# Folding the position-bias tiles of two steps into one of eight points with 16 rows each, ahead of the third layer of a small network

## The chip, the cores and the metric

The kernel runs on one core of a Trainium2 chip. The metric is the device time of one execution in microseconds (us); a comparison uses the median of several runs. Five engines work side by side, each through its own queue in order: PE (TensorE, matmuls into PSUM), DVE (VectorE), ACT (ScalarE), POOL (GpSimd) and SP (SyncE, which here only issues DMAs). DMAs are issued from SP's and POOL's queues and run on 16 DMA engines that all queues share; one that adds to its destination (an accumulating DMA) is issued from POOL. A trace of one profiled execution shows every instruction.

## The reference: what is computed

Four attention layers run one after the other on x of shape (2, 512, 32, 32), all in float32. Only the first, layer 0, is touched. It is a deformable attention: per image and group, 64 sampled key points, 1024 query pixels, and a bias that a small network (2 to 128 to 128 to 1) computes from the position of each query relative to each point:

```python
q = _gconv1x1(xn, qw)
...
pos = grid_q[:, :, None, :] - grid_kv[:, None, :, :]
bias = jnp.sign(pos) * jnp.log1p(jnp.abs(pos))
bias = jax.nn.relu(bias @ cpb_w1 + cpb_b1)
bias = jax.nn.relu(bias @ cpb_w2 + cpb_b2)
bias = (bias @ cpb_w3 + cpb_b3).reshape(b, GROUPS, H * W, Hd * Wd)
sim = jnp.einsum('bhid,bhjd->bhij', qh, kh) + bias
attn = jax.nn.softmax(sim, axis=-1)
out = jnp.einsum('bhij,bhjd->bhid', attn, vh)
...
out = jnp.einsum('bchw,oc->bohw', out, out_w) + out_b[None, :, None, None]
x = x + out
```

The network is evaluated 2 x 8 x 64 x 1024 times with 128 hidden units. Its second layer is a 128 x 128 product for each point and pixel, its third a product with one column.

## The kernel before

**Head pairs, steps and points.** Layer 0 works through 8 head pairs (`NT`; 2 images, 4 pairs of groups each, 128 points in a pair: one for each partition of `sim`). A pair has 32 *steps* (`NR`), a step 4 points, 256 steps in all (`steps`). For each point `first` (L491, one DVE instruction, L502) forms the 128 hidden values for 1024 pixels from two small tables, into a ring of 12 tiles of which 8 lie in the buffer `wa`; it runs 8 points (`AHEAD`, two steps) ahead of the step that uses them.

**Second layer.** `second` (L512) computes 32 of the 128 outputs (a *part*) for all four points at once: point p goes to rows 32p to 32p+31 of the PSUM tile `z`, so four matmuls of 32 columns run side by side in the array (L519). There are three `z` buffers, which all other small products of layer 0 share. ACT evicts `z` with the relu into an `h2` tile (L527). A step does the parts in the order 1, 0, 3, 2.

**Folding four parts into one.** The third layer is linear and has one output, so what follows the relu may be added up before it, if |w3| is multiplied into the second layer and the hidden units are sorted so that the sign of w3 is uniform over a row of a part. `joined` (L530) adds two parts on DVE, with a sign per row in `turn` (L532): part 0 takes in part 1 in the same step, part 2 takes in part 3 in the next step. An accumulating DMA on POOL's queue (L763) then adds the second sum onto the first. What remains of a step is one tile `joins[i]` of 128 rows: 4 points, 32 rows each.

**Third layer.** After every fourth step `third` (L537) multiplies the last four of these tiles with `w3`, a narrow matrix of signs whose slice `w3[:, 28 - r : 60 - r]` puts the four points of a tile on rows r to r+3 of a 32-row quarter of `sim`. Four tiles go to the four quarters, side by side, in two halves of 512 pixels: 8 matmuls (L542), each written as two records in the trace. 8 calls fill a pair's `sim`; then `scores` adds the attention scores, and `behind` (a chain of generators, advanced twice a step) does `finish` (softmax, L558), `offsets` (a depthwise convolution for the points of the pair after next, ACT products and DVE reduces, L310) and `samples` (L404) between the steps of the next pair.

**Order.** `in_order` keeps each engine's instructions in program order. The loop (L749) issues, for each of four k in a step: a `first`, a `second`, at k = 1 the join of the previous step and its DMA, at k = 1 and 3 one piece of `behind`, at k = 3 the join of this step. SP's queue has the table loads (`load_tabs`, L473, two every four steps, used from the second step of the next chunk on, after `scale_tab` on ACT) and the few other loads; after the last step also the 4 MB of `mlp_w1` (L751), which go into the buffer `wa`. POOL's queue has the accumulating DMAs and now and then a memset.

**Buffers.** `h2p` (8, part 0), `h2b` (3, part 2) and `h2q` (3, parts 1 and 3) hold the tiles. At the start the same pools hold weights (`qkwbd`, `nat`) for the *folds* (L690): products of weight matrices of a later layer that PE does before the steps begin.

**End of layer 0.** The last two steps are joined by DVE instead of the DMA (L765). `finish` of the last pair has nothing to hide behind; it does parts of the output projection (`project_out`, L624) for chunks 0 and 1 while the softmax runs, and the rest after.

Of the kernel before, what the change touches and what calls it, by code (L numbers as in the profile page):

```python
# [11 lines left out]
F32 = mybir.dt.float32  # L12
AF = mybir.ActivationFunctionType
ALU = mybir.AluOpType
AX = mybir.AxisListType
# [3 lines left out]
P = 128  # L19
B, C, H, W = 2, 512, 32, 32  # L20
HW = H * W
# [7 lines left out]
HID = 4 * C  # L29
EPS = 1e-5  # L30
BN_S = float(1.0 / np.sqrt(np.float32(1.0 + EPS)))
RCH = 4


_PC = [
# [44 lines left out]
def kernel(ctx: ExitStack, tc: tile.TileContext, a: dict, out: bass.AP):  # L80
# [56 lines left out]
    def layer0(l0, fold_d, t2_b, o2_b):  # L137
# [1 line left out]
        l0.enter_context(in_order(tc))  # L139
        one = l0.enter_context(tc.tile_pool(name="att1", bufs=1))  # L140
        two = l0.enter_context(tc.tile_pool(name="att2", bufs=2))
        h2p = l0.enter_context(tc.tile_pool(name="att_h2", bufs=8))
        h2b = l0.enter_context(tc.tile_pool(name="att_h2b", bufs=3))
        h2q = l0.enter_context(tc.tile_pool(name="att_h2q", bufs=3))
        dram = l0.enter_context(tc.tile_pool(name="l0dram", bufs=1, space=DRAM))
# [4 lines left out]
        def zt(shape, name):  # L150
            return ps_z.tile(shape, F32, name=name, tag="z")
# [10 lines left out]
        qkw = h2p.tile([P, 2, NPAIR, P], F32, name="qkwbd", tag="h2")  # L162
# [56 lines left out]
        b2h = one.tile([P, 4], F32, name="b2h")  # L219


        w3 = one.tile([P, 60], F32, name="w3")
        nc.gpsimd.memset(w3, 0.0)

        def magnitude(dst, src):
            nc.vector.tensor_scalar(dst, src, -1.0, None, ALU.mult)
# [2 lines left out]
        def bias_weights():  # L229
            sort = h2b.tile([P, 7, P], F32, name="sort", tag="h2")  # L230
            row, below, w2t = [sort[:, k, :] for k in range(3)]
            perm = sort[:, 3:, :].rearrange("p b (r u) -> p b r u", u=32)
            few = one.tile([P, 24], F32, name="few")
# [233 lines left out]
            nc.vector.tensor_add(simbias[t], pb, col("cpb_b3"))  # L467

        NR = 32
        NCH = NR // RCH  # L470
# [12 lines left out]

        def scale_tab(c, ax):
# [5 lines left out]

        def first(p):  # L491

            i, point = divmod(p, 4)
            chunk, quad = divmod(i, 4)
# [7 lines left out]
            nc.vector._custom_dve(  # L502
                TENSOR_ADD_SAT,
                out=h1.rearrange("p (y x) -> p y x", x=W),
                in0=tx[:, quad, point, :].unsqueeze(1).to_broadcast([P, H, W]),
                in1=ty[:, quad, point, :].unsqueeze(2).to_broadcast([P, H, W]),
                s0=float(np.finfo(np.float32).max),
                s1=0.0,
            )
            return h1  # L510

        def second(h1s, part):  # L512

            z = zt([P, HW], "z")
            lo = BLOCK[part]
            for half in range(2):
                n = slice(half * HALF, (half + 1) * HALF)
                for point in range(4):
                    nc.tensor.matmul(  # L519
                        z[point * 32 : point * 32 + 32, n],  # L520
                        cpb_w2[:, lo : lo + 32],
                        h1s[point][:, n],
                        start=True,
                        stop=True,
                    )
            h2 = (h2q if part % 2 else h2b if part else h2p).tile([P, HW], F32, name="h2", tag="h2")
            nc.scalar.activation(h2, z, AF.Relu, bias=b2h[:, part : part + 1])  # L527
            return h2

        def joined(parts, part):  # L530
            h2 = parts.pop(part)
            nc.vector.scalar_tensor_tensor(  # L532
                h2, h2, turn[:, part // 2 : part // 2 + 1], parts.pop(part + 1), ALU.mult, ALU.add
            )
            return h2

        def third(sim, r, h2s):  # L537

            for half in range(2):
                n = slice(half * HALF, (half + 1) * HALF)  # L540
                for quad, h2 in enumerate(h2s):
                    nc.tensor.matmul(  # L542
                        sim[quad * 32 : quad * 32 + 32, n],
                        w3[:, 28 - r : 60 - r],
                        h2[:, n],
                        start=(r == 0),
                        stop=False,
                    )

        def scores(t, sim):  # L550
# [3 lines left out]
                nc.tensor.matmul(sim[:, n], kqs[t], xs[b][:, pr, n], start=False, stop=True)  # L554

        oTs = {}

        def finish(t, sim):  # L558

# [29 lines left out]
            pps = []  # L589
# [22 lines left out]
            if pr < NPAIR - 1:  # L612
                return
            for m in range(CC):
                if m < len(pps):
# [133 lines left out]
        for i in range(steps + 2):  # L749
            if i == steps:  # L750
                (w1s,) = load_w(wa, "wa", [a["mlp_w1"]])  # L751
            for k, part in enumerate((1, 0, 3, 2)):
                if i % 4 == 1 and k % 2 == 0 and i // 4 + 1 in tabs_of:
                    scale_tab(i // 4 + 1, k // 2)
                p = 4 * i + AHEAD + k
                if p < 4 * steps:
                    h1s[p] = first(p)
                if i < steps:
                    parts.setdefault(i, {})[part] = second([h1s[4 * i + point] for point in range(4)], part)
                if k == 1 and i - 1 in parts:  # L760
                    other = joined(parts.pop(i - 1), 2)
                    if i < steps:
                        nc.gpsimd.dma_start(out=joins[i - 1], in_=other, accum_op=ALU.add)  # L763
                    else:
                        nc.vector.tensor_add(joins[i - 1], joins[i - 1], other)  # L765
                if k % 2:
                    next(behind, None)
                if k == 3 and i < steps:
                    joins[i] = joined(parts[i], 0)
            for point in range(4):  # L770
                h1s.pop(4 * i + point, None)
            if i >= 5 and i % 4 == 1:
                t, r = divmod(i - 5, NR)
                if r == 0:
                    sim = ps_s.tile([P, HW], F32, name="sim")
                third(sim, r, [joins.pop(i - 5 + j) for j in range(4)])
                if r == NR - 4:
                    assert next(behind, None) is None
                    scores(t, sim)
                    behind = chain(  # L780
                        finish(t, sim),
                        offsets(t + 2) if t + 2 < NT else iter(()),
                        samples(t + 1) if t + 1 < NT else iter(()),
                    )
        drain(behind)
        return w1s

# [856 lines left out]
```

## Time and profile before

| quantity | us |
| --- | --- |
| median of 3 runs | 3558.87 (3557.84 to 3559.7) |
| profiled execution | 3558.93 |
| span of its trace (first to last instruction) | 3556.6 |
| first matmul of the second layer (L519) starts | 61.9 |
| last one starts | 2061.0 |
| second layer on PE, busy (16384 records) | 1804.6 |
| third layer on PE, busy (1024 records) | 124.5 |
| second pair of heads, 32 steps (300.8 to 548.3) | 247.6, of which DVE busy 233.4, ACT 180.2 |
| `first` on DVE, each | 1.22 |
| join on DVE, each | 1.28 |

The kernel spends some 2000 us of its span in the steps of layer 0. "Busy" counts the time in which at least one instruction of a group runs, so four matmuls side by side count once. A wait in front of an instruction is given as idle time with the instruction that ended it (the releaser). Waits of PE are what sets the time here, as it is hardly ever idle.

### The profile page before, as it was taken

The page shows a single profiled execution, that of the slowest core. Times are in us where ns is not written, and L with a number is a line of the kernel's source. Part 1 is how long each engine was busy: PE and PEld are TensorE (multiplying, and loading weights), DVE is VectorE, ACT ScalarE, POOL GpSimd, SP SyncE. Part 2 cuts the span into 40 slices and gives each one's busy share as a digit, 9 for nine tenths or more (in the row PEclk, how much of TensorE's full clock was granted, in tenths as well). Part 3 has the DMA queues.
Part 4 walks back from the last instruction along what each step waited for, and adds up shares of the span by engine and source line. Part 5 has one row for each costly group of instructions (what it writes and reads, how often), then busy time and mean ns, then how long its engine had stood idle before and what let it go on. Part 6 is the DMA issues. An engine that isn't in the chain of part 4 may idle for free.

```text
span 3556.6 us, 58202 instructions
## 1 busy us (share of the span) xinstructions
PE 3522.7 (99%) x24777; PEld 1469.1 (41%) x24777; DVE 2479.0 (70%) x2720; ACT 1760.6 (50%) x2478; POOL 278.1 (8%) x326
## 2 busy tenths in 40 slices
PE   9999999999999999999999989999999999999999
PEld 4333333333333233333333349999533333444443
DVE  6999998998996998999999934554255364130223
ACT  4767866867764867767776621122144233111111
POOL 0111111111110111111111100000001000000000
PEclk9999999999999999999999999999999999999999
DMA  5454444554442444444444430000200000000000
GB/s 167 95 92 83 81 96 88 90 90 84 91 94 53 87 91 82 96 84 87 94 85 88 85 112 13 10 10 13 80 1 0 1 1 0 15 0 0 6 30 25
DMA packets 135964, 213.46 MB, mean 60 GB/s; under 512 B 14992, under 2 KB 93200, under 8 KB 134928
## 3 DMA queue, kind: packets, MB, share of 16 engines
q0 software_dynamic: 36720, 133.71, 19.9%
q1 hardware_dynamic: 98832, 75.41, 8.8%
q8 instruction: 197, 3.23, 0.4%
q14 instruction: 71, 0.58, 0.0%
q10 hardware_dynamic: 144, 0.52, 0.0%
HBM read 64.12 MB, written 10.75 MB: 21 GB/s over the span
## 4 chain that ended last, share of the span: by engine, by line
PE 96%; DVE 1%; ACT 1%; issue 1%; DMA 0%; POOL 0%; POOLq 0%; DVEq 0%; ACTq 0%
PE z L519 49%; PE pw L135 6%; PE pm L1243 5%; PE pma L135 5%; PE pmv L135 5%; PE pmb L135 4%; PE score L1354 4%; PE sim L542 3%; PE score L135 3%; PE pv L1402 3%; PE ppr L1274 2%; PE pmp L135 2%; PE pp L628 2%; PE pf L135 1%; PE pma L1216 1%
## 5 line engine op out<-in xcount | busy, mean ns | idle before, releaser
L527 ACT ACTIVATE h<-z,b2h 128x1024 f32<-128x1024 f32 x1024 | 1135.0, 1114 | 575.3 <-PE z L519 570.5
L519 PE MATMUL z<-wa,cpb_w 128*32 128x512 f32 x10880 | 1195.9, 593 | 3.3 <-ACT h L527 3.3
L502 DVE CUSTOM_DVE_ANT_1 wa<-tab,tab 128x1024 f32<-128x1024 f32 x680 | 801.1, 1221 | 23.6 <-PE z L519 19.5
L519 PEld LDWEIGHTS z<-wa,cpb_w 128*32 128x32 f32 x10880 | 346.4, 110 | 808.5 <-issue 730.8
L532 DVE SCALAR_TENSOR_TENSOR h<-h,turn,h 128x1024 f32<-128x1024 f32 x512 | 655.9, 1281 | 25.7 <-ACT h L527 25.6
L519 PE MATMUL z<-h,cpb_w 128*32 128x512 f32 x5504 | 608.7, 593 | 0.9 <-ACT h L527 0.9
L502 DVE CUSTOM_DVE_ANT_1 h<-tab,tab 128x1024 f32<-128x1024 f32 x344 | 405.3, 1221 | 15.0 <-PE z L519 14.9
L763 POOL DMA_DIRECT2D h<-h x255 | 219.5, 861 | 1801.2 <-DVE h L532 1308.8
L519 PEld LDWEIGHTS z<-h,cpb_w 128*32 128x32 f32 x5504 | 175.8, 110 | 408.4 <-issue 372.8
L1355 ACT ACTIVATE p<-score 128x1024 f32<-128x1024 f32 x144 | 139.6, 1021 | 184.8 <-PE score L1354 184.8
L135 PE MATMUL pw<-p,vT 128*128 128x512 f32 x512 | 221.8, 593 | 1.3 <-DVE y L1460 1.3
L1285 DVE TENSOR_TENSOR acc<-acc,p 128x2048 f32<-128x2048 f32 x56 | 128.8, 2300 | 105.1 <-ACT p L1355 57.8
L1138 ACT COPY p<-pma 128x128 f32<-128x128 f32 x70 | 18.6, 266 | 304.2 <-PE pma L135 304.2
L1287 DVE TENSOR_TENSOR acc<-p 128x2048 f32<-128x2048 f32 x12 | 27.5, 2292 | 183.6 <-ACT p L1489 110.0
L135 PEld LDWEIGHTS pw<-p,vT 128*128 128x128 f32 x512 | 97.0, 190 | 122.6 <-issue 121.0
L1130 DVE TENSOR_TENSOR upper<-pma,p 128x256 f32<-128x256 f32 x70 | 29.6, 423 | 163.5 <-ACT p L1138 163.5
L542 PE MATMUL sim<-h,w 128*32 128x512 f32 x1024 | 124.5, 598 | 5.8 <-DMA h<-h 5.8
L1354 PE MATMUL score<-q,k 64*128 64x512 f32 x512 | 127.2, 615 | 0.0
L1243 PE MATMUL pm<-hc,wa 128*64 128x512 f32 x512 | 122.4, 603 | 0.0
L1402 PE MATMUL pv<-p,vT 128*64 128x512 f32 x512 | 121.4, 595 | 0.0
L135 PE MATMUL score<-t,hc 128*128 128x512 f32 x256 | 110.2, 592 | 0.0
L1460 DVE TENSOR_TENSOR y<-pw,r 128x512 f32<-128x512 f32 x32 | 21.8, 682 | 115.5 <-PE pw L135 115.5
(300 smaller groups left out, 3110.2 us busy)
## 6 DMA issues: line engine op xcount, KB each, us to landing
h<-h POOLq DMA_DIRECT2D x255, 512.0 KB, 5.0
tab<-slog_d SPq DMA_DIRECT2D x128, 256.0 KB, 7.0
wa<-in_qkv_w SPq DMA_DIRECT2D x8, 768.0 KB, 6.2
xt<-in_xt SPq DMA_DIRECT2D x8, 512.0 KB, 5.8
wa<-in_mlp_w SPq DMA_DIRECT2D x4, 1024.0 KB, 9.7
wb<-in_mlp_w SPq DMA_DIRECT2D x16, 256.0 KB, 5.6
x_d<-x SPq DMA_DIRECT2D x32, 128.0 KB, 1.8
out<-x SPq DMA_DIRECT2D x16, 256.0 KB, 2.0
```

Of the source, the lines that this page charges most:

```text
L135: nc.tensor.matmul(pm, w, m, start=(k == 0), stop=(k == len(pairs) - 1))
L502: nc.vector._custom_dve(TENSOR_ADD_SAT, out=h1.rearrange("p (y x) -> p y x", x=W), in0=tx[:, quad, point, :].unsqueeze(1).to_broadcast([P, ...
L519: nc.tensor.matmul(z[point * 32 : point * 32 + 32, n], cpb_w2[:, lo : lo + 32], h1s[point][:, n], start=True, stop=True,)
L527: nc.scalar.activation(h2, z, AF.Relu, bias=b2h[:, part : part + 1])
L532: nc.vector.scalar_tensor_tensor(h2, h2, turn[:, part // 2 : part // 2 + 1], parts.pop(part + 1), ALU.mult, ALU.add)
L542: nc.tensor.matmul(sim[quad * 32 : quad * 32 + 32, n], w3[:, 28 - r : 60 - r], h2[:, n], start=(r == 0), stop=False,)
L763: nc.gpsimd.dma_start(out=joins[i - 1], in_=other, accum_op=ALU.add)
L1243: nc.tensor.matmul(pm[at : at + wide], w[:, k, lo + at : lo + at + wide], h[k][:, n], start=(k == 0), stop=(k == CC - 1),)
L1285: nc.vector.tensor_add(acc, acc, p)
L1354: nc.tensor.matmul(sc[:, part, :], ks[part][r, left[part]], qs[part][r, n], start=True, stop=True)
L1355: nc.scalar.activation(p[:, :, n], sc, AF.Exp, scale=scale)
L1402: nc.tensor.matmul(pv[part * 64 : part * 64 + 64, n], vT[:, ls, lo : lo + 64], lp[:, part, n], start=(ls == 0), stop=(ls == 7),)
```

## The change

A tile `joins[i]` has 4 points of 32 rows. The new kernel folds the 32 rows of a point into 16 and puts two steps into one tile: rows 2u get the sum of rows 2u and 2u+1 of the even step, rows 2u+1 the same sum of the odd step. Three transfers do it for each pair of steps (e even, o = e + 1):

- in step e + 2, at k = 0: an accumulating DMA on POOL's queue adds the odd rows of `joins[e]` onto its even rows (64 rows of 4 KB);
- in step e + 3, at k = 0: a DMA on SP's queue copies the even rows of `joins[o]` into the odd rows of `joins[e]`;
- in step e + 3, at k = 3: an accumulating DMA on POOL's queue adds the odd rows of `joins[o]` onto these.

The last two steps (254 and 255) aren't folded. `third` now takes four tiles of eight points each, with a sign matrix of 8 columns (`w3`, 56 wide); the last call takes three such tiles and the two tiles of four points through the old matrix (`w3_4`). It runs once for eight steps, at k = 1 of the third step after the last pair has begun its folds (`due`), instead of once for four steps after the fourth k. So `finish` of a pair begins a step and a half later too.

So that eight consecutive points fall into one tile, the tables are loaded in another order (`RCH` 8: two runs of 8 points for a chunk of 16 points, instead of four runs of 4), of the same size.

The pools: part 0 of even steps in `h2p` (now 6), of odd steps in a new pool `h2j` (3), which also holds `qkwbd` at the start.

At the top four small DVE operations build the new sign matrix, and one more piece of the folds goes ahead of the bias weights and the first offsets (`advance(fold_steps, 3)`). At the end the first two of four products of chunk 1's projection are issued right after the last step, and `finish` of the last pair keeps only chunk 0's early part; `pa` reuses `pt`'s buffer.

```diff
-RCH = 4
+RCH = 8
...
-        h2p = l0.enter_context(tc.tile_pool(name="att_h2", bufs=8))
+        h2p = l0.enter_context(tc.tile_pool(name="att_h2", bufs=6))
+        h2j = l0.enter_context(tc.tile_pool(name="att_h2j", bufs=3))
...
-                nc.vector.tensor_copy(w3[r, 28 + point : 29 + point], w3sign[r, 1:2])
+                nc.vector.tensor_copy(w3_4[r, 28 + point : 29 + point], w3sign[r, 1:2])
+
+            odd, eighth = few[:, 24:25], few[:, 25:26]
+            nc.vector.tensor_reduce(odd, ident[:, 1:P:2], AX.X, ALU.add)
+            nc.vector.scalar_tensor_tensor(eighth, odd, 4.0, cs("py", 0), ALU.mult, ALU.subtract)
+            nc.vector.tensor_scalar(w3[:, 24:32], row[:, 0:8], eighth, 0.0, ALU.add, ALU.is_equal)
+            nc.vector.tensor_scalar(w3[:, 24:32], w3[:, 24:32], w3sign[:, 1:2], None, ALU.mult)
...
-                tab = two.tile([P, 4, RCH, 32], F32, name=f"tab{ax}")
-                nc.sync.dma_start(out=tab, in_=src[:, rc * RCH : (rc + 1) * RCH, :].partition_broadcast(P))
+                tab = two.tile([P, 2, RCH, 32], F32, name=f"tab{ax}")
+                q, r = rc % 2 * 2, rc // 2 * RCH
+                nc.sync.dma_start(out=tab, in_=src[q : q + 2, r : r + RCH, :].partition_broadcast(P))
...
-            h2 = (h2q if part % 2 else h2b if part else h2p).tile([P, HW], F32, name="h2", tag="h2")
+            ring = h2q if part % 2 else h2b if part else h2j if i % 2 else h2p
+            h2 = ring.tile([P, HW], F32, name="h2", tag="h2")
...
-        def third(sim, r, h2s):
+        def third(sim, r, h2s, fours=()):
...
-                for quad, h2 in enumerate(h2s):
+                ways = [(quad, w3[:, 24 - r : 56 - r], h2) for quad, h2 in enumerate(h2s)]
+                for k, h2 in enumerate(fours):
+                    ways.append((3, w3_4[:, 28 - r - 4 * k : 60 - r - 4 * k], h2))
+                for k, (quad, w, h2) in enumerate(ways):
                     nc.tensor.matmul(
...
+                        sim[quad * 32 : quad * 32 + 32, n], w, h2[:, n], start=(r == 0 and k < 4), stop=False
                     )
...
-                pps = [zt([P, HW], "pp") for _ in range(2)]
-                for m in range(2):
-                    project_out(pps[m], m, range(NPAIR - 1 - m), oT)
-            pa = zt([P, 8, P], "pa")
+                pps.insert(0, zt([P, HW], "pp"))
+                project_out(pps[0], 0, range(NPAIR - 1), oT)
+            pa = pt if last else zt([P, 8, P], "pa")
...
-        advance(fold_steps, 2)
+        advance(fold_steps, 3)
...
             if i == steps:
                 (w1s,) = load_w(wa, "wa", [a["mlp_w1"]])
+
+                pps.append(zt([P, HW], "pp"))
+                project_out(pps[0], 1, range(NPAIR - 2), oTs[B - 1])
...
+                if i >= 2 and i % 2 == 0 and k == 0 and i < steps:
+                    nc.gpsimd.dma_start(out=joins[i - 2][0:P:2], in_=joins[i - 2][1:P:2], accum_op=ALU.add)
+                if i >= 3 and i % 2 and k == 0 and i < steps:
+                    nc.sync.dma_start(out=joins[i - 3][1:P:2], in_=joins[i - 2][0:P:2])
+                if i >= 3 and i % 2 and k == 3 and i < steps:
+                    nc.gpsimd.dma_start(out=joins[i - 3][1:P:2], in_=joins.pop(i - 2)[1:P:2], accum_op=ALU.add)
...
+                due = i - 11 if i < steps else i - 9
+                if k == 1 and due >= 0 and due % 8 == 0:
+                    t, r = divmod(due, NR)
...
+                    eights = [joins.pop(due + j) for j in range(0, 8 if i < steps else 6, 2)]
+                    third(sim, r, eights, [joins.pop(steps - 2 + j) for j in range(2)] if i >= steps else ())
+                    if r == NR - 8:
...
-            if i >= 5 and i % 4 == 1:
-                t, r = divmod(i - 5, NR)
...
-                third(sim, r, [joins.pop(i - 5 + j) for j in range(4)])
-                if r == NR - 4:
```

More of the change, by code (lines that the diff above doesn't have):

```diff
@@ L161, in layer0 @@
         nc.scalar.dma_start(out=xs[0][:, 0, :], in_=a["x"][0, 0:P, :])
-        qkw = h2p.tile([P, 2, NPAIR, P], F32, name="qkwbd", tag="h2")
+        qkw = h2j.tile([P, 2, NPAIR, P], F32, name="qkwbd", tag="h2")
         vw = one.tile([P, NPAIR, P], F32, name="vwbd")
@@ L219, in layer0 @@
         b2h = one.tile([P, 4], F32, name="b2h")
-        w3 = one.tile([P, 60], F32, name="w3")
-        nc.gpsimd.memset(w3, 0.0)
+        w3 = one.tile([P, 56], F32, name="w3")
+        w3_4 = one.tile([P, 60], F32, name="w3_4")
+        for w in (w3, w3_4):
+            nc.gpsimd.memset(w, 0.0)
         def magnitude(dst, src):
@@ L232, in bias_weights @@
             perm = sort[:, 3:, :].rearrange("p b (r u) -> p b r u", u=32)
-            few = one.tile([P, 24], F32, name="few")
+            few = one.tile([P, 26], F32, name="few")
             minus = few[:, 0:1]
@@ L469, in layer0 @@
         NR = 32
-        NCH = NR // RCH
+        NCH = 2 * NR // RCH
         tabs_of = {}
@@ L491, in first @@
         def first(p):
-            i, point = divmod(p, 4)
-            chunk, quad = divmod(i, 4)
+            chunk, quad = divmod(p, 2 * RCH)
+            quad, point = divmod(quad, RCH)
             if quad == 0 and point == 0:
@@ L510, in first, with second @@
             return h1
-        def second(h1s, part):
+        def second(i, h1s, part):
             z = zt([P, HW], "z")
@@ L535, in joined @@
             return h2
-        def third(sim, r, h2s):
+        def third(sim, r, h2s, fours=()):
             for half in range(2):
                 n = slice(half * HALF, (half + 1) * HALF)
-                for quad, h2 in enumerate(h2s):
+                ways = [(quad, w3[:, 24 - r : 56 - r], h2) for quad, h2 in enumerate(h2s)]
+                for k, h2 in enumerate(fours):
+                    ways.append((3, w3_4[:, 28 - r - 4 * k : 60 - r - 4 * k], h2))
+                for k, (quad, w, h2) in enumerate(ways):
                     nc.tensor.matmul(
[L543 to L547, printed above, removed]
+                        sim[quad * 32 : quad * 32 + 32, n], w, h2[:, n], start=(r == 0 and k < 4), stop=False
                     )
@@ L556, in layer0 @@
         oTs = {}
+        pps = []
         def finish(t, sim):
@@ L588, in finish @@
             last = t == NT - 1
-            pps = []
             if last:
-                pps = [zt([P, HW], "pp") for _ in range(2)]
-                for m in range(2):
-                    project_out(pps[m], m, range(NPAIR - 1 - m), oT)
-            pa = zt([P, 8, P], "pa")
+                pps.insert(0, zt([P, HW], "pp"))
+                project_out(pps[0], 0, range(NPAIR - 1), oT)
+            pa = pt if last else zt([P, 8, P], "pa")
             for i in range(8):
@@ L614, in finish @@
             for m in range(CC):
-                if m < len(pps):
+                if last and m < len(pps):
                     pp = pps[m]
@@ L758, in layer0 @@
                 if i < steps:
-                    parts.setdefault(i, {})[part] = second([h1s[4 * i + point] for point in range(4)], part)
+                    four = [h1s[4 * i + point] for point in range(4)]
+                    parts.setdefault(i, {})[part] = second(i, four, part)
+                if i >= 2 and i % 2 == 0 and k == 0 and i < steps:
[4 more added lines that the diff above has]
+                    nc.gpsimd.dma_start(out=joins[i - 3][1:P:2], in_=joins.pop(i - 2)[1:P:2], accum_op=ALU.add)
                 if k == 1 and i - 1 in parts:
@@ L769, in layer0 @@
                     joins[i] = joined(parts[i], 0)
+                due = i - 11 if i < steps else i - 9
+                if k == 1 and due >= 0 and due % 8 == 0:
+                    t, r = divmod(due, NR)
+                    if r == 0:
+                        sim = ps_s.tile([P, HW], F32, name="sim")
+                    eights = [joins.pop(due + j) for j in range(0, 8 if i < steps else 6, 2)]
+                    third(sim, r, eights, [joins.pop(steps - 2 + j) for j in range(2)] if i >= steps else ())
+                    if r == NR - 8:
+                        assert next(behind, None) is None
+                        scores(t, sim)
+                        behind = chain(
+                            finish(t, sim),
+                            offsets(t + 2) if t + 2 < NT else iter(()),
+                            samples(t + 1) if t + 1 < NT else iter(()),
+                        )
             for point in range(4):
                 h1s.pop(4 * i + point, None)
-            if i >= 5 and i % 4 == 1:
-                t, r = divmod(i - 5, NR)
-                if r == 0:
-                    sim = ps_s.tile([P, HW], F32, name="sim")
-                third(sim, r, [joins.pop(i - 5 + j) for j in range(4)])
-                if r == NR - 4:
[L778 to L784, printed above, removed]
         drain(behind)
```

## The prediction

> **What bounds the kernel now.** I read the page first (busy shares, then the costliest groups), then the timeline of PE and of DVE inside layer 0, then the DMA issues, then the chain of waits at the end of layer 0.
>
> ```profile
> span 3556.6 us, 58202 instructions
> PE 3522.7 (99%) x24777; PEld 1469.1 (41%) x24777; DVE 2479.0 (70%) x2720; ACT 1760.6 (50%) x2478; POOL 278.1 (8%) x326
> ...
> L532 DVE SCALAR_TENSOR_TENSOR h<-h,turn,h 128x1024 f32<-128x1024 f32 x512 | 655.9, 1281 | 25.7 <-ACT h L527 25.6
> ...
> L542 PE MATMUL sim<-h,w 128*32 128x512 f32 x1024 | 124.5, 598 | 5.8 <-DMA h<-h 5.8
> ```
>
> PE is the bound: 99% busy, and the third layer (L542) waited for its DMA only once. The trace writes each fp32 matmul as two records, so 1024 records are 64 calls of `third` with 8 matmuls. The timeline of PE gives the true price of a call:
>
> ```profile
> 526.02 7.05 PE L519 MATMUL z<-wa,cpb_w 128*32 128x512 f32 x64
> 532.88 1.90 PE L542 MATMUL sim<-h,w 128*32 128x512 f32 x16
> 534.60 7.05 PE L519 MATMUL z<-wa,cpb_w 128*32 128x512 f32 x64
> ```
>
> From start to start a step of the second layer takes 532.88 - 526.02 = 6.86 us and a `third` 534.60 - 532.88 = 1.72 us (1.90 has the tail that the next group overlaps). Before, four steps take 4 x 6.86 + 1.72 = 29.16 us.
>
> DVE is close behind, at 70% of the span only because the later layers spare it. A step without other work, and one with the reduce of the offsets (L341):
>
> ```profile
> 519.42 2.35 DVE L502 CUSTOM_DVE_ANT_1 wa<-tab,tab 128x1024 f32<-128x1024 f32 x2
> ...
> 526.36 2.36 DVE L502 CUSTOM_DVE_ANT_1 h<-tab,tab 128x1024 f32<-128x1024 f32 x2
> ...
> 639.14 2.35 DVE L502 CUSTOM_DVE_ANT_1 wa<-tab,tab 128x1024 f32<-128x1024 f32 x2
> ...
> 644.88 0.97 DVE L341 TENSOR_REDUCE products<-products 128x64 f32<-128x448 f32 x1
> ...
> 646.96 2.35 DVE L502 CUSTOM_DVE_ANT_1 h<-tab,tab 128x1024 f32<-128x1024 f32 x2
> ```
>
> Four `first` and two joins take 6.94 us, with a reduce 7.82 us. So DVE is slower than PE's bare step (6.86) and catches up during each `third`.
>
> **The change, part by part.**
>
> *Third layer, removed.* 32 calls instead of 64: 32 x 1.72 = 55.0 us. The last call has five ways instead of four; the fifth shares a column group with the fourth, so it runs behind it: 2 halves x 0.43 us (a quarter of 1.72, one group) = 0.86 us, or twice that if both records count. Net -54 us, all on the path, because PE has no other wait there.
>
> *DVE, the new neighbour.* Eight steps now take PE 8 x 6.86 + 1.72 = 56.6 us (7.08 a step) and DVE 55.5 us without reduces. The cover that let DVE catch up is halved. How far may it fall behind? Today the second join of a step ends 3.8 us after PE's end of that step where DVE keeps pace, and at most 8.2 us after (step 8 of the first head pair: PE ends at 127.98, the join at 136.16), and PE's next steps show no loss. After the change six steps in a row carry a reduce: each adds 7.82 - 6.86 = 0.96 us, less one `third` at the first of them: 3.8 + 5 x 0.96 = 8.6, and the five small operations after them (680.81 to 681.62, 0.8 us) make 9.4, less about 0.4 us for PE's own small matmul there: 9.0. In the first head pair, where two calls of `third` fall away among its first ten steps, about 9.9. If PE starts waiting just above 8.2, that is 0.8 us for each of six pairs and 1.7 us once, 6.5 us; a further z buffer of slack (one part, 1.7 us) would hide all. Between 0 and 7, I take 3. ACT's two table scalings (L489, 0.76 us each) no longer fall in the step with the `third`; its 0.4 us surplus over PE in such a step is inside that 7.
>
> *Three transfers for each pair of steps, added.* POOL adds odd rows onto even rows (64 rows of 4 KB), SP copies the even rows of the odd step into the odd rows of the even step, POOL adds again. 126 to 127 of each.
>
> ```profile
> h<-h POOLq DMA_DIRECT2D x255, 512.0 KB, 5.0
> tab<-slog_d SPq DMA_DIRECT2D x128, 256.0 KB, 7.0
> ...
> kq<-qk SPq DMA_DIRECT2D x4, 256.0 KB, 3.5
> ```
>
> The accumulates took 19.9% of 16 engines: 708 us / 255 = 2.78 us each, so 5.0 - 1.39 = 3.6 us is my estimate for half of one; `kq<-qk` is the same copy, 64 rows of 4 KB, at 3.5. With DVE 6 us behind, and 0 at PE's end of the even step: its accumulate is issued at 6.0 and lands at 11.0, the fold lands at 14.6; the odd step's accumulate goes at 12.9, lands at 17.9; the copy at 21.4, the second fold at 25.0. `third` stands half way through the fifth step after it: 4 x 6.86 + 3.4 = 30.9. Slack 5.9 us for the last pair; the other three are earlier. Behind POOL's second fold stands the next even step's first fold, which itself waits until later; behind SP's copy stand the table loads, which have three steps. POOL's issue costs 0.86 us each, three in 13.7 us. The engines get fuller: the share in layer 0 is 0.46 to 0.49, and 5.6 us more for each 13.7 (two folds and a copy at 1.39 each, plus what they collide with) makes about 0.8. I take a wait of 0, and 0 to 0.5 us a call, 16 us, as the bound from a fold that collides with a 2.78 us accumulate twice over.
>
> The Trainium skill ("DMA: Bandwidth & Descriptors", Rules for kernel authors) speaks against this part: two transfers on disjoint partition halves gain nothing, since both use the same 16 engines; one of 128 partitions is better. Its fixed cost of about 2.0 us per DMA (same page, Anatomy of one DMA) would make the three legs shorter than the rows do, and the sum the same. The rule is right on bandwidth, but the price here is latency, which the slack covers.
>
> *More semaphores on PE.* Each of the first four matmuls of a call now waits for three DMA semaphores instead of one; two of them become instructions of their own. The trace shows such an instruction (L519, PEldq) at 51 ns: 8 x 51 = 0.41 us a call at most, 0 where the matmuls ahead hide it, as they do at L519. 32 calls: 0 to 13 us; I take 2, near the hidden end.
>
> *Top.* One fold (8 records of L135, 3.5 us) moves ahead of the bias weights; four DVE operations of 0.16 us come in. `first` starts some 4 us later, but PE reaches the second layer only at 61.94, 12 us after the first four tiles would be there (45.3 + 4 + 4.7 = 54). The granted clock is 0.50 from 32 to 42 us either way. 0, between -2 and +2.
>
> *Tail.* Two thirds of the projection of chunk 1 (8 records, 3.4 us) move from the softmax gap into the wait for the last tiles.
>
> ```profile
> 2057.76 10.42 DMA h<-h
> ...
> 2068.22 3.63 PE sim L542 x12
> 2071.85 2.52 PE sim L554 x4
> ```
>
> That accumulate took 10.42 us beside the 4 MB of `mlp_w1`, and PE's clock fell to 0.51 between 2066 and 2073. The last fold now lies behind it in POOL's queue and lands 1.4 us or more later (+1.4). The fifth way adds nothing more. PE's wait, from 2061.4, shrinks from 5.8 to some 4 us; if the clock holds, 12 records and the scores cost 1.3 + 1.7 instead of 6.1 us (-3); if not, the longer call costs double. The softmax gap (8.59 us of PE work, DVE ready about 0.7 us before its end) loses its cover: -0.7, or +1 if PE is cold after it. Together -4 to +5; I take +1.
>
> The skill ("TensorE: Matmul & The Clock Gate", Why this matters for your kernels) asks for no PE gaps over about 3 us, or the clock halves. The row agrees that 5.8 us was enough; by the rule both new gaps (4 and 3.4 us) can still cost it, and the tail would be +5.
>
> *Sum.* -54 + 3 + 0 + 2 + 0 + 1 = -48 us on the span of 3556.6: 3508.6. The profiled execution took 3558.93, 2.3 more than its span, and lies 0.06 from the median 3558.87. So 3511. The ends, not all at once: -54 - 6 = 3499 and -54 + 7 + 13 + 5 + some of the 16 = 3535.
>
> **Rivals.**
>
> *DVE becomes the bound.* For: 6.94 against 6.86 us, and at 7.08 only 0.14 us a step to recover in. Against: over a head pair of 32 steps DVE has 14 us of idle time now (247.6 us a pair), and PE gives up 6.9 of it. If half the gain stays in DVE waits, 27 us: 3532.
>
> *The transfer chain is late (slower).* The last pair's second fold has 5.9 us to spare. For: engines go from half full to about 0.8, tab loads of the same size take 7.0 us, and the accumulate in the tail shows 10.42. If copy and second fold take 8.5 us each (between these two), they land at 17.9 + 17 = 34.9, PE waits 4.0 us in each of 32 calls: +128, about 3640. It decides from 6.5 us a leg; slower than before it is from about 7.2. Against: 5.0 is a stable median (4.5 at least), and full rows of 4 KB are nothing like the table's 512 B packets.
>
> *It doesn't do what it says*: if PE ran the new call slower, for instance with the waits breaking the four-fold overlap throughout, a call of 3.4 us would leave nothing: 3559.
>
> **How the numbers follow.** The forecast has 0.72, DVE 0.13, the late chain 0.12, no effect 0.03. Changes under 0.2% (7 us) can't be told from none. Faster: 0.72 + 0.13 + 0.01 = 0.86; same 0.02; slower 0.12. The likeliest case alone spans 3499 to 3526; with the DVE case in, 3499 to 3536 leaves out the late chain and little else.
>
> **What would show it.** L542's successor with some 516 records and 1.7 us a call; its idle time near 5 us, not 30 or more, on DMA; steps of 6.87 us; z waiting for ACT in the steps with the reduce, a few us in all; DVE's idle time in layer 0 down by about 50 us. Wrong: idle time of PE on `h<-h` in most calls, folds landing after 7 us, or DVE at full share over whole head pairs with PE gaps.

## The result, and the profile after

| | before | after |
| --- | --- | --- |
| median of 4 runs, us | 3558.61 (3557.84 to 3559.7) | 3510.25 (3507.89 to 3513.06) |
| profiled execution, us | 3558.93 | 3512.09 |
| span of its trace, us | 3556.6 | 3510.3 |

The ratio is 0.9864, with a 95% interval of 0.9847 to 0.9881: the change made the kernel 48.4 us faster. 3511 had been forecast.

These lines are from the page and the groups of instructions of the changed kernel. In a group, the busy time and the mean ns of one stand behind the first bar, the idle time of the engine before it and what ended it behind the second; a DMA issue ends with the median us to its landing. A *fold* is from here on one of the two accumulating transfers that add odd rows onto even rows (L776 the first, L780 the second), the *copy* is the transfer between them (L778); L784 is the 512 KB accumulate that was there before.

```profile
span 3510.3 us, 58708 instructions
PE 3470.8 (99%) x24269; PEld 1452.0 (41%) x24269; DVE 2474.9 (71%) x2724; ACT 1761.3 (50%) x2478; POOL 494.2 (14%) x581
...
DMA  5776676666674676666766710001100000000000
...
L543 DVE SCALAR_TENSOR_TENSOR h<-h,turn,h 128x1024 f32<-128x1024 f32 x512 | 653.9, 1277 | 13.5 <-ACT h L538 13.1
...
L776 POOL DMA_DIRECT2D h<-h x127 | 108.3, 853 | 402.4 <-DMA h<-h 397.7
...
h<-h POOLq DMA_DIRECT2D x255, 512.0 KB, 4.8
h<-h POOLq DMA_DIRECT2D x254, 256.0 KB, 4.8
tab<-slog_d SPq DMA_DIRECT2D x128, 256.0 KB, 6.0
h<-h SPq DMA_DIRECT2D x127, 256.0 KB, 2.3
```

PE is as full as before (99%) and the span 46.3 us shorter, so the gain is PE work that is gone. DVE joined and formed the same tiles and found half the idle time before its joins (13.5 us; L532 had 25.7). The DMA row shows 6s and 7s where layer 0 had 4s and 5s, yet the 512 KB accumulates land no later (4.8 us, before 5.0). POOL now also waits for transfers of its own (397.7 us before L776); what stands behind in its queue are the next accumulates, and experiment 4 measures what that costs.

The timeline of PE shows one call of the new third layer, and a wait that the old kernel did not have (in brackets the idle time and its releaser):

```profile
625.71 1.90 PE L556 MATMUL sim<-h,w 128*32 128x512 f32 x16
627.42 3.62 PE L529 MATMUL z<-h,cpb_w 128*32 128x512 f32 x32
...
669.41 3.64 PE L529 MATMUL z<-h,cpb_w 128*32 128x512 f32 x32 [0.29 <-ACT h L538]
```

From start to start a call takes 627.42 - 625.71 = 1.71 us, as before, now once in eight steps. The wait of 0.29 us returns once in each of five head pairs, at the same place in the pair.

The start times of the matmuls cut each trace into four stretches: the *top* until the first second-layer matmul, the *steps* until the last one, the *tail* from there to the next part of the kernel (`pmp`), and the *rest*.

| us | before | after | difference | forecast |
| --- | --- | --- | --- | --- |
| top | 61.94 | 61.67 | -0.3 | 0 |
| steps | 1999.06 | 1947.13 | -51.9 | -50.0 |
| tail | 48.39 | 55.13 | +6.7 | +1.9 |
| rest | 1447.24 | 1446.37 | -0.9 | 0 |
| span | 3556.64 | 3510.29 | -46.3 | -48 |

(The forecast's sum, sorted: 32 calls times 1.72 less, 3 for DVE and 2 for semaphores fall in the steps; the fifth way of the last call, 0.86, and the 1 for the tail fall in the tail.) A mid-kernel head pair takes 241.2 us instead of 247.56.

The tail is the part that went otherwise. The critical chain of the changed kernel there (start us, us, what):

```profile
2009.39 3.63 PE pp L637 x8
2013.02 0.98 PE sim L556 x4
2014.00 6.09 issue
2020.09 5.99 PE sim L556 x16
2026.08 1.93 PE sim L564 x4
```

PE does the projection that was moved there (L637), starts the last third-layer call with its first two tiles and then stands for 6.09 us in front of the third one: the folded tile of steps 252 and 253. The timeline of the same kernel tells what is late, and the windows what it does to the granted clock, the share of full speed at which PE's clock ran (busy time and, in brackets, the instructions of PE, PEld, DVE, ACT and POOL; then granted clock, DMA share, GB/s):

```profile
2004.20 0.47 SPq L778 DMA_DIRECT2D h<-h  x1
...
2004.77 2.31 SPq L119 DMA_DIRECT2D wa<-in_mlp_w  x4
...
2007.04 0.83 POOL L780 DMA_DIRECT2D h<-h  x1 [0.61 <-DMA h<-h]
```

```profile
2018.00:2022.00 4.00, 1.91 (x10) 0.89 (x12) 0.00 (x0) 0.00 (x0) 0.00 (x0) 0.50 0.86 341
2022.00:2026.00 4.00, 4.00 (x11) 0.71 (x5) 0.00 (x0) 0.00 (x0) 0.00 (x0) 0.65 0.00 2
```

Over the whole run the fold and the accumulate took this long to land:

```profile
L780 POOL DMA_DIRECT2D h<-h x127: 830/907/1222, 94.7 to 2007.0; - x127
DMA to landing us min/median/max: 3.2/6.0/13.0
...
L784 POOL DMA_DIRECT2D h<-h x255: 852/862/1528, 75.0 to 2005.6; - x128
DMA to landing us min/median/max: 4.5/4.8/11.7
```

The last fold (L780) is issued 2.3 us behind the 4 MB load of `mlp_w1`; PE goes on 13.0 us after that issue (2020.09 - 2007.04), where the median fold lands in 6.0. The last accumulate (L784), issued 1.5 us ahead of it, takes 11.7 us for 4.8; both longest landings are these last ones. The granted clock is then 0.50 and 0.65, and the 16 records take 5.99 us.

### The profile page after: what moved, and what is told of

It reads as the page before. It is cut to its first block, busy times and chain, and to the rows that moved or that the text cites. A ratio compares the mean times of both kernels' runs of the same rounds, so it can differ in the third digit from the quotient of the medians.

```text
span 3510.3 us, 58708 instructions
## 1 busy us (share of the span) xinstructions
PE 3470.8 (99%) x24269; PEld 1452.0 (41%) x24269; DVE 2474.9 (71%) x2724; ACT 1761.3 (50%) x2478; POOL 494.2 (14%) x581
## 4 chain that ended last, share of the span: by engine, by line
PE 90%; DVE 6%; ACT 2%; issue 2%; DVEq 0%; POOL 0%; ACTq 0%; POOLq 0%
PE z L529 43%; PE pw L135 6%; PE pm L1266 5%; PE pma L135 5%; PE pmv L135 5%; PE pmb L135 4%; PE score L1377 4%; PE score L135 3%; PE pv L1425 3%; DVE wa L512 2%; PE sim L556 2%; DVE h L543 2%; PE ppr L1297 2%; PE pmp L135 2%; PE pp L637 1%
## 5 line engine op out<-in xcount | busy, mean ns | idle before, releaser
L543 DVE SCALAR_TENSOR_TENSOR h<-h,turn,h 128x1024 f32<-128x1024 f32 x512 | 653.9, 1277 | 13.5 <-ACT h L538 13.1
L784 POOL DMA_DIRECT2D h<-h x255 | 224.9, 882 | 1080.5 <-DVE h L543 703.2
L776 POOL DMA_DIRECT2D h<-h x127 | 108.3, 853 | 402.4 <-DMA h<-h 397.7
L780 POOL DMA_DIRECT2D h<-h x127 | 126.2, 993 | 50.2 <-DMA h<-h 42.6
L1068 POOL TENSOR_SCALAR hc<-x,sc,sh 128x1024 f32<-128x1024 f32 x16 | 28.1, 1767 | 704.6 <-DVE sh L1064 507.9
```

Of the source, the lines that this page charges most:

```text
L543: nc.vector.scalar_tensor_tensor(h2, h2, turn[:, part // 2 : part // 2 + 1], parts.pop(part + 1), ALU.mult, ALU.add)
L780: nc.gpsimd.dma_start(out=joins[i - 3][1:P:2], in_=joins.pop(i - 2)[1:P:2], accum_op=ALU.add)
```

## The experiments

Each kernel starts from the changed one unless it says otherwise. Where a single execution stands against another, the stretches of the table are compared and not the totals.

**1. The load of `mlp_w1` issued later.** Theory: the tail's loss is this load, which shares the 16 engines with the last accumulate and the last fold.

```diff
+            if t == NT - 1:
+                w1_late.extend(load_w(wa, "wa", [a["mlp_w1"]], queue=nc.scalar))
...
-                (w1s,) = load_w(wa, "wa", [a["mlp_w1"]])
```

It is issued from ACT's queue in `finish` of the last pair, behind the eviction of the scores.

> The changed kernel, with the 4 MB of mlp_w1 loaded through ACT's queue behind the last simb instead of through SP's queue right after the last step. Theory A (the end of layer 0 lost 6.7 us because the last pair's second fold shares the DMA engines with mlp_w1: issued at 2007.0, PE waits for it until 2020.1, then runs at half clock): the second fold lands within 4 to 5 us of its issue, PE's 6.1 us gap in front of the last third-layer call goes, the clock stays at 1.0 there, and the kernel is 8 to 12 us faster than the changed one, about 3500. Theory B (the gap comes from the chain of three transfers by itself, whatever else moves): the gap stays at 4 us or more and the time within 3 us of the changed kernel's 3510. Theory C (PE waits for DVE's last join and add): gap unchanged, 3510.

Ratio to before 0.9844 (0.9828 to 0.986), median 3502.25 us. The tail is 45.59 us instead of 55.13, the steps are unchanged (1947.08). The critical chain of this kernel at the end of layer 0:

```profile
2010.10 3.63 PE pp L640 x8
2013.73 3.57 PE sim L556 x20
2017.30 1.93 PE sim L564 x4
```

The fold lands 4.8 us after its issue. The call runs through, all 20 records in 3.57 us at full clock (1.00 in this stretch). So the load beside the last transfers cost 9.5 us, wait and clock together.

**2. The same on the kernel before.** If the load had hurt both alike, it would not explain a difference.

> The kernel before, with the same later load of mlp_w1. Theory A: the last plain accumulate, which took 10.42 us beside the load, takes about 5; PE's gap of 5.8 us goes and so do the 6.8 us of half clock: 5 to 8 us faster than before, 3551 to 3554. It also says how much of the later load's worth belongs to the change (the rest was there before). Theory B: within 2 us of before.

Ratio 0.9986 (0.9977 to 0.9996). The tail falls from 48.39 to 44.93 us, 3.5 us, less than expected (the medians differ by 5.0): without the load PE still waits 2.0 us, now for DVE's addition (L768):

```profile
2064.26 1.23 DVE h L768
2065.50 0.04 issue
2065.54 2.68 PE sim L542 x10
```

(DVE adds the second sum of step 255 alone. That of step 254 still goes by a DMA, the last of the 255 accumulates; that both last steps are joined by DVE, as the description of the kernel has it, is not so.) So the old kernel lost 3.5 us to the load and the new one 9.5; without it the two tails are alike (44.93 and 45.59).

**3. The old order of the projection in the tail.** Both products of chunk 1 back into the softmax gap, the time in which PE has no other work than this while the last pair's softmax runs.

```diff
-                pps.insert(0, zt([P, HW], "pp"))
-                project_out(pps[0], 0, range(NPAIR - 1), oT)
-            pa = pt if last else zt([P, 8, P], "pa")
+                pps.extend(zt([P, HW], "pp") for _ in range(2))
+                for m in range(2):
+                    project_out(pps[m], m, range(NPAIR - 1 - m), oT)
+            pa = zt([P, 8, P], "pa")
...
-                pps.append(zt([P, HW], "pp"))
-                project_out(pps[0], 1, range(NPAIR - 2), oTs[B - 1])
```

> The changed kernel with the order of the output projection at the end of layer 0 as before (both early chunks in the softmax gap, none in front of the last third-layer call). If moving 3.4 us of projection in front of the call was worth anything, this is 1 to 3 us slower than the changed kernel; if the move only uncovered PE in the softmax gap (2.7 us of waiting for the normalised weights and another drop of the clock after it), it is 2 to 4 us faster, with PE's gap in front of the call longer by 3.4 us (9.5 instead of 6.1). The steps of layer 0 (1947.1 us) do not change.

Ratio 0.9865 (0.9848 to 0.9881), as the changed kernel. The tail is 54.10 us, 1.0 less. The work only changes the wait that it fills, as the chain shows:

```profile
2009.46 0.84 PE sim L556 x4
2010.31 9.70 issue
2020.01 6.24 PE sim L556 x16
```

3.6 us more wait here (9.70 against 6.09), and in the changed kernel 2.7 us of wait in the softmax gap, where PE now runs out of work before DVE is ready (`pt` waits for L597, below). The move itself shows no gain.

**4. The three transfers left out.** The third layer reads the even steps' tiles unfolded; those of the odd steps are left out of the bias.

```diff
-                    nc.gpsimd.dma_start(out=joins[i - 2][0:P:2], in_=joins[i - 2][1:P:2], accum_op=ALU.add)
+                    pass
...
-                    nc.sync.dma_start(out=joins[i - 3][1:P:2], in_=joins[i - 2][0:P:2])
+                    pass
...
-                    nc.gpsimd.dma_start(out=joins[i - 3][1:P:2], in_=joins.pop(i - 2)[1:P:2], accum_op=ALU.add)
+                    joins.pop(i - 2)
```

> The changed kernel without the three transfers for each pair of steps; the third layer reads the unfolded tiles, so odd steps drop out of the bias. Theory 'hidden' (the transfers cost nothing in the steps): the second layer's first to last matmul takes 1947 us as with the transfers, within 1 us; only the end changes, as for the later load. Rival 'late chain or contention': the steps get shorter by more than 2 us, up to the 3.1 us that the steps are above the sum 1999.1 - 32 x 1.72 = 1944.0.

The steps take 1946.97 us against 1947.13, every head pair the same within 0.04. So 381 transfers, 100 MB, cost 0.2 us in the steps: they are hidden. In the tail PE still waits, for a plain accumulate that takes 10.84 us beside the load:

```profile
2001.24 10.84 DMA h<-h
2012.08 0.14 issue
2012.21 5.29 PE sim L556 x14
```

The tail is 51.06 us here. So of the 9.5 us that the load costs the changed kernel 4.1 come with the folds (55.13 - 51.06), and 5.5 (51.06 - 45.59) are lost without them; this is read from one execution.

**5. The third layer one step earlier.** This takes 6.9 us from the slack of the chain of transfers (and lets `finish` begin that much earlier).

```diff
-                due = i - 11 if i < steps else i - 9
+                due = i - 10 if i < steps else i - 9
```

> The changed kernel with the third layer one step (6.9 us) sooner after its last pair of steps. In the changed kernel the second fold of the last pair is issued 9.0 to 14.5 us before the call, and such a fold takes 6.0 us to land in the median, so 3 to 8 us are to spare. Theory 'the slack is real': in 24 of the 32 calls the fold is now issued only 2 to 4.2 us ahead and PE waits 2 to 4 us each, in the 8 others (those with 14 us) nothing: 50 to 100 us in all, 3560 to 3610, and the steps stretch by as much. Rival 'the transfers are far from mattering': under 10 us slower, 3510 to 3520.

The steps take 2053.87 us, 106.7 more: slower than before (3613.79 against 3552.33 us for a run of before on the same chip), and a little more than the 50 to 100 us expected. PE's waits in this kernel (us in total, times, longest), and the chain of one of them:

```profile
PE sim L556 <- DMA h<-h: 61.2, 26, 4.4
...
PEld sim L556 <- DMA h<-h: 88.5, 30, 5.3
```

```profile
570.88 1.12 issue
572.00 6.63 DMA h<-h
578.62 0.04 issue
578.67 1.90 PE sim L556 x10
```

In this call the fold lands at 578.62, 2 us after PE has run dry. The weight loads of 30 calls waited. By the start times of PE's matmuls in the trace, 62.4 of the 106.7 us are additional waits of PE (68.6 us in the steps against 6.2), nearly all in front of L556. The other 44.3 us are longer distances between starts without a wait: 25.4 in the second layer, and 19.0 in the calls, which now run in pieces (73.0 us for 31 calls against 54.1). The clock was halved 11 times within the steps, 48 us in all; the 24 us that half speed loses in them are about the 25.4.

**6. Each call of the third layer issued twice.** Its bias counts twice.

```diff
-                for k, (quad, w, h2) in enumerate(ways):
+                for k, (quad, w, h2) in enumerate(ways + ways[:4]):
```

> The changed kernel with every third-layer call issued twice over (the bias is added twice). If PE's own matmul time is what a call costs, each of the 31 calls within the steps takes 1.72 us more: the steps go from 1947.1 to 1947.1 + 53.3 - (0 to 3, the small waits that DVE's lag caused) = 1997 to 2000 us, that is back to the kernel before (1999.1). If DVE or the transfers had set the pace of the changed kernel, part of it would be hidden: under 1985.

The steps take 2000.12 us, 53.0 more; 31 calls inside them times 1.72 are 53.3. So a call costs its PE time in full, neither hidden nor lengthened by its waits. The time is that of before (1999.06) to 1.1 us, with all transfers running.

**7. Five of six reduces of the offsets left out**, so the offsets of the sampling points come from fewer products.

```diff
                     if kx == 5:
-                        n = 7 if ky else 6
+                        if ky < 5:
+                            continue
+                        n = 6
```

> The changed kernel without five of the six reduces of the offsets on DVE in each head pair (the offsets then come from one row of taps). DVE's work falls by about 5 x 0.9 us a pair. Theory 'DVE's lag costs the last few us': the steps shorten from 1947.1 toward 1944, by 2 to 3.5 us, and the second join of a step never ends more than about 6 us after PE. Rival 'it is something else' (ACT's table scalings, the extra semaphores of the third layer): under 1 us.

The steps take 1945.06 us, 2.07 less. The list of PE's waits for ACT has this line in the changed kernel:

```profile
PE z L529 <- ACT h L538: 6.2, 15, 0.5
```

and this one without the reduces:

```profile
PE z L531 <- ACT h L540: 4.2, 9, 0.5
```

The kernel before had 4.3 us in 9 waits, so the reduces make the six that are gone here: the 0.29 us of the five pairs, and 0.51 us in the first pair.

**8. The old order at the top**: `advance(fold_steps, 2)`.

> The changed kernel with two pieces of the folds ahead of the bias weights as before, not three. The forecast said nothing is won or lost at the top (between -2 and +2): the second layer starts at 61.94 in the kernel before and 61.67 in the changed one. So it starts at 61.9 here, within 0.5, whatever the first tiles on DVE do. Rival: the move hides a loss from the longer start of the new sign matrix; then it starts later than 62.5.

The first second-layer matmul starts at 60.64 us (61.67 with the new order), outside of what was expected, but between executions this figure goes from 57.5 to 62.4 us (last section). The steps take 1947.03 us, the run 3510.18 us: no effect that can be told.

**9. Late load and old projection order together**, and, on the same chip, the changed kernel and the late load alone again.

> The changed kernel with the later load of mlp_w1 and the old order of the projection at the end together. With the later load PE has no gap in front of the last third-layer call except DVE's last join and add (some 4 us after the last second-layer matmul), and with the old order the projection fills the softmax gap, where the later load alone left PE waiting 2.7 us for the weights and at half clock for 3.4 us. Theory A: the end of layer 0 (last second-layer matmul to the first of the MLP) takes 43 to 46 us, against 45.6 with the later load alone and 55.1 in the changed kernel: the sum of both, 0 to 2 us faster than the later load alone. Rival: the old order only moves the gap back in front of the call (4 us longer wait, clock down): 1 to 3 us slower than the later load alone.

> The changed kernel unaltered, on the same chip and in the same rounds as the two others, so that their ratios to it can be read. 0.986 of the kernel before; the later load should be 0.9970 to 0.9980 of it (7 to 10 us).

> The changed kernel with the later load of mlp_w1 alone, again, beside the two others: 7 to 10 us faster than the changed kernel; the two sets of times do not overlap by more than the 5 us by which single executions of one kernel differ (half-clock windows before the second layer starts fall differently).

| kernel | median us | ratio to before | tail us |
| --- | --- | --- | --- |
| changed | 3511.38 (3507.99 to 3512.12) | 0.9868 (0.9853 to 0.9883) | 55.30 |
| late load | 3502.58 (3496.63 to 3502.75) | 0.9842 (0.9829 to 0.9856) | 45.45 |
| late load, old projection order | 3499.66 (3496.44 to 3501.07) | 0.9837 (0.9824 to 0.9851) | 43.89 |

The last is the fastest kernel of the study, 11.7 us below the changed one. Of this 8.8 us are the load's. The remaining 2.9 us lie within the spread of the runs; by the traces 1.6 us of the tail belong to the order. The critical chain of this kernel:

```profile
2008.38 1.24 DVE h L788
2009.62 0.04 issue
2009.67 2.76 PE sim L556 x12
2012.43 1.93 PE sim L564 x4
...
2015.55 1.09 PE pt L584 x8
2016.64 8.59 PE pp L641 x20
2025.23 0.87 PE pa L610 x8
```

The projection fills the softmax gap again (L641 up to `pa`, with no wait between), and the last wait of the last call ends on DVE's addition instead of on a fold.

## Why the prediction was right, point by point

*Third layer, removed: -54.* Right. L556 has half the records at 1.71 us a call, and doubling the calls (experiment 6) brings back 53.0 us of 53.3. Only the fifth way of the last call, 0.86 us or twice that, was the double: in experiment 1 that call takes 3.57 us at full clock, 1.86 more than one of four ways.

*DVE, the new neighbour: +3, between 0 and 7.* Right in size: the steps lost 55.0 - 51.9 = 3.1 us. Counted from PE's start on the next step, the second join of a step ends at most 8.6 us later in five of the pairs with reduces (forecast 9.0; in the second pair PE starts at 423.99 and the join ends at 432.51) and 9.4 in the first (9.9). Where 8.2 had cost nothing, 8.5 costs 0.29 us and 9.4 costs 0.51. The lag alone does not decide it: in the fifth pair 9.4 us cost nothing, where PE had 2.2 us of other work in the step. Experiment 7 gives 2.07 of the 3.1 to the reduces. One part of the reason is corrected by experiment 6: with each call twice as long DVE has all its old cover, and the waits of 0.27 to 0.29 us stay. They come from the run of reduces between two calls, whatever the calls are worth. Some 1.0 us of the 3.1 was not traced to a cause. Which buffer passes DVE's lag on to ACT and PE was not tried.

*Three transfers: 0, between 0 and 16.* Right: 0.2 us (experiment 4). The legs differ from the forecast. The copy takes 2.3 us where the nearest row (3.5) had been taken, the second fold 6.0 where half an accumulate (3.6) had been; it is issued right behind a 512 KB accumulate of the same queue. Their sum is 8.3 us for 7.1. From the landing of a call's last fold to its first matmul the trace shows 1.6 to 8.7 us in 30 of the 31 calls within the steps, in half of them under 4; 5.9 had been forecast, so the chain was nearer to being late than the forecast had it. Two sums on the way were off without harm. POOL issues four transfers in 13.7 us, not three, since both steps have their accumulate. The share of the DMA engines became 0.67 (from 300.8 to 548.3 us; before 0.47), not 0.8.

*More semaphores on PE: +2, between 0 and 13.* Mis-sized: 0. The call from start to start is 1.71 us with its waits, of which the trace has four instructions a call (129 in all, 51 ns at the median), not eight.

*Top: 0.* Right within the scatter (experiment 8).

*Tail: +1, between -4 and +5.* Mis-sized, and beyond its end: +6.7 with the fifth way, 1.9 forecast. The term that failed is "lands 1.4 us or more later (+1.4)". It adds half an accumulate's time on the engines behind an accumulate that was taken to land as before, although the row quoted beside it showed what the load does to such a transfer (10.42 us). The accumulate took 11.7 us, and the fold landed 2.8 us behind it, 13.0 us after its issue. Counted from the start of the last second-layer matmul, PE could go on after 11.3 us, before after 7.2: 4.1 us later instead of 1.4. PE's wait, forecast to shrink to 4 us, stayed at 6.09 although 3.6 us of work had been put in front of it, and the clock was halved for 6.8 us, from 2018 on. The scores so end 19.2 us after the last second-layer matmul starts, before 13.4: +5.8; the other 0.9 us are the softmax gap, forecast at -0.7 to +1. The Trainium skill, "TensorE: Matmul & The Clock Gate" (Why this matters for your kernels), warns of gaps above about 3 us; the gap of 6.09 us has the clock at 0.50 behind it, and the +5 that the forecast gave by this rule was nearer than the +1 it took.

The total was better than its terms. On the span the errors were -2 for the semaphores, +4.8 for the tail and -1.2 for the rest and the top, with 0.1 for DVE +1.7 together (3508.6 forecast, 3510.3 measured); the median then lies at the span of the profiled execution, where 2.3 had been added for what lies around it. That 3511 was hit to 0.8 us is luck; what the runs bear out is the 51.9 us of the steps, for 50.0.

*The rivals.* DVE did not become the bound: in a pair from the middle of the run it still has 8.3 to 9.2 us of idle time; 14 less 6.9 had been worked out. The late chain was the right rival to fear: experiment 5, one step less, cost 106.7 us and made the kernel slower than before. The call that runs slower is excluded by experiment 6.

## What to carry to other kernels

Work that a full engine no longer does is worth its start-to-start time in the timeline, and the transfers in its stead were free here because the whole chain fitted into the distance between producer and consumer; that distance is to be laid out in steps and checked by taking one away. Price a transfer by what shares the queue and the engines with it at that moment, not by its median: the fold took 6.0 us in the steps at the median and 13.0 us beside a 4 MB load. A load that is needed late should wait for the last short transfer on the critical path, above all where the wait also halves PE's clock.

## What the runs showed of the hardware

**The phase of the clock at the start.** The granted clock is halved in stretches of 3.41, 6.83 or 10.24 us. Before the second layer starts, such stretches add up to 3.4 us in the executions of experiments 4 and 9 (first second-layer matmul at 57.51 and 58.22 us) and to 10.2 in those of before and after (61.94 and 61.67). After and experiment 4 do the same work up to there; half of the 6.8 us more at half clock is 3.4 of the 4.2 us between them. The Trainium skill, "TensorE: Matmul & The Clock Gate" (What's actually happening), describes a window of 3413 ns that runs free of the kernel's start; the lengths here agree. So single executions can differ by some 4 us with nothing changed (the four of the changed kernel in experiment 9 go from 3507.99 to 3512.12), and they were compared by stretches here. That the phase is the cause was not tried by itself.

**Shorter waits can halve it too.** In the changed kernel this wait of 2.68 us, shorter than the page's 3, is followed by a clock of 0.57 in the next 4 us:

```profile
2038.12 1.66 PE L606 MATMUL pt<-cst,at 128*128 128x128 f32 x8 [2.68 <-DVE at L597]
```

```profile
2038.00:2042.00 4.00, 3.88 (x12) 2.50 (x12) 0.00 (x0) 1.01 (x1) 0.00 (x0) 0.57 0.00 0
```

The wait of 2.03 us in experiment 2 has a clock of 0.51 behind it (2066.5 to 2070). Not every short wait does this: in experiment 5, whose longest wait in the steps was 4.4 us by the matmuls and 5.3 by the weight loads, 26 waits of the matmuls brought 11 stretches at half clock, and in experiment 9 none follows the waits of 1.5 and 1.2 us at the end of layer 0.
